# Placing the last context squares ahead of the position-bias table in a fused Perceiver kernel

## Chip, cores and metric

The kernel runs on one core of one Trainium2 chip, as a single launch. The metric is the device time of that launch in microseconds (us), the median of the runs shown.

## What is computed

The reference is a four-level Perceiver: an activation x of 16 batches x 64 tokens x 256 features goes through twelve residual blocks, several of which attend to a context of 16 x 1601 rows of 256 features. Cut to the blocks around the change:

```python
x = x + _L0_attn_ref(_layernorm(x), ...)           # 4 encoder layers, linear attention
x = x + _L0_ffn_ref(_layernorm(x), ...)            # 8 experts, two per token, capacity 160
x = x + _L1_xattn_ref(_layernorm(x), ctx_1024, ...)
...
x = x + _L3_attn_ref(_layernorm(x), ..., L3_attn_rel_emb)

# _L0_ffn_ref
probs = softmax(x @ gate_w.T); top2_w, top2_idx = top_k(probs, 2)
h = relu(einsum('th,ehf->tef', x, W1) + b1); y = einsum('teh,ehf->tef', h, W2) + b2
# _L1_xattn_ref
Pn = ctx * rsqrt(mean(ctx * ctx, -1) + eps) * input_norm_w
# _L3_attn_ref
att = q @ k.T / sqrt(D) + rel_emb[buckets]         # then causal mask, softmax
```

Three pieces of this meet at the change: the **squares** (the sums of squares of the context rows, which only the cross-attention of level 1 needs), the **routes** (which two experts each token goes to, and its place in the expert's table), and the **position bias** (a table of 128 x 1024 values that only the last attention of the kernel needs).

## The kernel before

The program is written in Python with a tile framework that turns tile accesses into semaphore waits. Each engine runs its own instruction list in order. Where `keep_in_program_order` is called (through the wrapper `Written`, line 51, and through `mm` and `tr`, lines 2617 and 2630, while `pinned` is set), the list has the order of the source. A tile that takes over the memory of an earlier tile waits until the last reader of that memory is done (pools with `reuse_waits="tile"`).

`l0_attn` works on the 1024 tokens as two halves, a and b, of four 128-token tiles; its steps are generators that are advanced by hand with `go`. The squares are such a generator as well: `context_squares` (line 2635) loads the context in 48 pieces from the queue of ScalarE (ACT) and emits one `Square` activation with a row sum per 128 x 256 block, 208 in all. `squares(n)` (line 515) emits the next n of them; they are sprinkled through the feed-forward layers, and `squares(999)` emits whatever is left. By then every piece has been loaded and 8 squares are left.

At the end of `l0_attn` (lines 971 to 1008) stand, in this order:

- four calls of `route` (line 836). Each transposes a pair of token tiles, copies them on ACT into `hT`, computes the gate logits on TensorE (PE), ranks them on VectorE (DVE), and has GpSimd (POOL) scatter the token rows into the DRAM table `taken` with four indirect DMAs (line 894). The fourth call, line 983, has nothing beside it.
- the position bias (lines 984 to 1004): 8 matmuls that put the causal mask into PSUM, 128 small matmuls of one-hot bucket rows with the embedding, which finish the tile `pb`, and 16 copies on ACT from `pb` to `kept`. Line 1006 writes the table to DRAM from POOL's queue.
- the rest of the squares (line 1007).

`l0_ffn` (line 1028) comes next. On the queue of SyncE (SP) stand, in order: 8 loads of 256 KB with the weights of experts 4 to 7 (line 1057, into tiles `w12` that take over memory of `l0_attn`), 4 loads of the row of `b2` (line 1062), the first load of gathered tokens `xs` from `taken` (line 1066), 4 loads of `xw` (line 1069), and the other 3 loads of `xs`. The first of the weight loads goes to memory in which the context pieces lay. The first `xs` load waits for all 16 scatters. PE then transposes `xs` and `xw` (`turn`, line 1071), DVE and ACT copy the result to `xsT` (lines 127 and 129), and the experts run: `hidden`, `out`.

DVE and ACT have other work ahead of these copies. DVE: `rms` (line 1214, which reads all the sums of squares), part of the gate softmax (L447), two steps on `rr` (L1216, L1217) and the rest of the softmax (L449 to L451). ACT: the square root of `rms` (L1215), a table load and the softmax's exponential (L448).

Of the kernel before, what the change touches and what calls it, by code (L numbers as in the profile page):

```python
# [64 lines left out]
class Sections:  # L65
# [415 lines left out]
    def l0_attn(self):  # L481
# [25 lines left out]
        with ExitStack() as ctx:  # L507
# [7 lines left out]
            def squares(n):  # L515
                for _ in range(n):
                    next(pieces, None)
# [31 lines left out]
            def norm(s, src, p):  # L549

                mv, r = s.by[p]
                V.reciprocal(r, r)
                for j in range(2):
                    t = 2 * p + j
                    V.tensor_scalar(s.n[:, t, :], src[:, t, :], mv[:, j, 0:1], r[:, j : j + 1], ALU.subtract, ALU.mult)
# [225 lines left out]
            def go(it, n=99):  # L781
                for _ in range(n):
                    if next(it, self) is self:
                        break
# [196 lines left out]
            measure(b, b.x, 1)  # L981
            norm(b, b.x, 1)
            go(route(b, 1))
            banks = ps_kv.tile([P, 2, 512], F32, tag="kv", name="pb")
            banks = [banks[:, 0], banks[:, 1], *(ps.tile([P, 512], F32, tag="tr", name="pb", bufs=2) for _ in range(2))]
            above = self.c("above")
# [17 lines left out]
                        A.copy(to[:, j], of)  # L1004
            self.position_bias = tc.dram_tile([P, 16 * S], F32, name="position_bias")
            nc.gpsimd.dma_start(self.position_bias, bias.rearrange("p r g s -> p (r g s)"))
            squares(999)
            self.pinned = False
        self.at_once.close()

# [1989 lines left out]
```

## Time and profile before

| what | value |
|---|---|
| median of 3 runs (lowest, highest) | 3731.08 us (3728.47, 3732.46) |
| profiled execution: its own time | 3730.16 us |
| profiled execution: span from first to last instruction | 3728.4 us |
| PE busy (matmul) / ACT busy / DVE busy, share of the span | 94% / 39% / 53% |
| mean granted PE clock | 0.979 |
| the 16 copies pb to kept on ACT | start 1343.49, together 3.47 us |
| the 8 last squares on ACT, with their 8 reads of the sum | 1346.99 to 1350.29 us |
| first weight load of line 1057 issued on SP | 1350.31 us |
| first expert matmul (hidden) on PE | 1364.72 us |

All times inside the execution are in microseconds from the start of the span. In a timeline row the columns are: start, duration, engine, source line, operation, output and inputs, shapes, count, and in brackets how long the engine had been idle and what released it. A line of a helper appears for many operations: L59 is the wrapper `Written`, L2619 the matmul helper, L2631 the transpose helper. SPq is the DMA-issuing queue of SP. A row "A <- B" among the waits says that A stood idle until B was done. PEclk is the clock that the TensorE was granted, as a share of full speed.

### The profile page before, as it was taken

What the parts mean: (1) busy time and instruction counts of PE and PEld (TensorE: products, weight loads), DVE (VectorE), ACT (ScalarE), POOL (GpSimd) and SP (SyncE); (2) the same over time, 40 slices, a digit from 0 to 9 for tenths busy, and PEclk for the clock granted to TensorE, in tenths of its full rate; (3) what the DMA queues carried; (4) which work ended last, traced back from release to release, by engine and by line L of the source; (5) the groups of instructions that cost most, each with busy time, mean ns of one, the idle gap of its engine ahead of it and who ended that gap; (6) DMA issues with size and microseconds to landing.
All of it is one profiled execution on the core that took longest, in us unless ns stands there. A gap on an engine that the chain in (4) does not pass through costs nothing.

```text
span 3728.4 us, 71203 instructions
## 1 busy us (share of the span) xinstructions
PE 3499.4 (94%) x31177; PEld 2200.2 (59%) x31192; DVE 1970.9 (53%) x3645; ACT 1461.2 (39%) x2093; POOL 1286.4 (35%) x784
## 2 busy tenths in 40 slices
PE   9999999998999979999988989999999889999997
PEld 4555555564665655555555666667767655555554
DVE  5344333436555635655656555577767765333445
ACT  2333333333444413444433443466666612111123
POOL 2555555552101113433422100577777630000002
PEclk9999999999999979999999999999999989999998
DMA  4111001101333345442101001211111004111550
GB/s 146 38 38 38 28 30 38 38 8 50 101 93 97 116 133 170 147 147 85 64 26 41 1 6 41 72 57 38 57 38 38 11 2 175 36 41 33 241 214 13
DMA packets 108071, 259.77 MB, mean 70 GB/s; under 512 B 9609, under 2 KB 76172, under 8 KB 105456
## 3 DMA queue, kind: packets, MB, share of 16 engines
q1 hardware_dynamic: 99040, 223.14, 16.8%
q10 hardware_dynamic: 6912, 27.27, 2.3%
q0 software_dynamic: 1808, 4.80, 0.5%
q8 instruction: 245, 4.01, 0.4%
q14 instruction: 66, 0.54, 0.0%
HBM read 248.85 MB, written 6.33 MB: 68 GB/s over the span
## 4 chain that ended last, share of the span: by engine, by line
PE 75%; DVE 13%; ACT 7%; issue 2%; DMA 1%; POOL 0%; SPq 0%; ACTq 0%; DVEq 0%; POOLq 0%
PE sc L2619 15%; PE pk L2619 15%; PE lin L2619 6%; PE acc L2619 6%; PE lin_t L2619 5%; ACT e L358 5%; PE pu L2619 4%; PE gate L2166 3%; PE up L2166 3%; PE lin L216 3%; PE pc L1786 3%; PE prz L2619 2%; PE gelu_t L1700 2%; PE turn L2631 1%; PE pa L2619 1%
## 5 line engine op out<-in xcount | busy, mean ns | idle before, releaser
L2548 POOL TENSOR_TENSOR tot<-tot,e 128x1024 f32<-128x1024 f32 (+1 forms) x340 | 803.2, 2362 | 373.3 <-ACT e L358 251.0
L299 DVE TENSOR_REDUCE m<-sc 128x4 f32<-128x2048 f32 x96 | 220.1, 2293 | 271.3 <-PE sc L2619 270.2
L1929 DVE SCALAR_TENSOR_TENSOR e<-sc,row_L_xattn_nbias,free 128x2048 f32<-128x2048 f32 x104 | 244.3, 2349 | 115.5 <-PE sc L2619 113.1
L1931 ACT ACTIVATE e<-e 128x2048 f32<-128x2048 f32 x104 | 198.7, 1911 | 245.8 <-DVE e L1929 245.8
L358 ACT ACTIVATE e<-sc 128x2048 f32<-128x2048 f32 x104 | 195.2, 1877 | 237.3 <-PE sc L2619 235.7
L2619 PE MATMUL sc<-qb,kT 32*128 32x128 f32 x6656 | 245.0, 283 | 36.2 <-DVE m L313 12.3
L2619 PEld LDWEIGHTS sc<-qb,kT 32*128 32x128 f32 x6656 | 206.1, 187 | 80.6 <-issue 22.4
L2619 PEld LDWEIGHTS acc<-e,v 128*32 128x32 f32 x6656 | 169.7, 109 | 105.3 <-issue 96.0
L2619 PE MATMUL acc<-e,v 128*32 128x128 f32 x6656 | 225.9, 276 | 4.7 <-ACT e L1932 4.7
L2619 PE MATMUL pk<-wv,cT 128*128 128x256 f32 x832 | 209.8, 394 | 0.0
L2619 PE MATMUL pk<-cT,wk 128*128 128x512 f32 (+1 forms) x512 | 206.2, 531 | 3.6 <-DVE rows L329 3.6
L1932 ACT ACTIVATE e<-e 128x2048 f32<-128x2048 f32 x104 | 198.7, 1911 | 3.2
L2619 PE MATMUL pk<-wkv,cT 128*128 128x256 f32 x832 | 196.3, 386 | 0.0
L2619 PE MATMUL pk<-cT,wkv 128*128 128x512 f32 (+1 forms) x512 | 194.9, 522 | 0.0
L2619 PEld LDWEIGHTS pk<-wv,cT 128*128 128x128 f32 x832 | 149.5, 190 | 76.4 <-issue 58.9
L2619 PEld LDWEIGHTS pk<-wkv,cT 128*128 128x128 f32 x832 | 153.2, 190 | 28.5 <-issue 4.3
L1786 PE MATMUL pc<-ew,eh 128*128 128x256 f32 x640 | 156.1, 386 | 0.0
L2170 ACT ACTIVATE g<-gate 128x512 f32<-128x512 f32 x68 | 40.6, 597 | 293.4 <-PE gate L2166 293.4
L2619 PE MATMUL sc<-kT,qb 32*128 32x512 f32 (+2 forms) x1536 | 138.9, 461 | 13.8 <-DVE m L299 2.3
L1319 POOL TENSOR_TENSOR e<-e,mx 128x512 f32<-128x512 f32 x96 | 81.9, 885 | 194.3 <-DVE mx L1318 194.3
L2619 PE MATMUL pu<-cn,e 128*64 128x257 f32 (+1 forms) x1248 | 141.6, 381 | 3.3 <-DMA cn<-in_ctx_n 1.8
L2171 DVE TENSOR_TENSOR hT<-up,g 128x512 f32<-128x512 f32 x68 | 47.0, 691 | 183.2 <-PE up L2166 183.2
(544 smaller groups left out, 6425.2 us busy)
## 6 DMA issues: line engine op xcount, KB each, us to landing
cT<-in_ctx_t SPq DMA_DIRECT2D x128, 832.0 KB, 6.4
cn<-in_ctx_n SPq DMA_DIRECT2D x32, 1664.0 KB, 11.9
piece<-in_ctx_n ACTq DMA_DIRECT2D x32, 640.0 KB, 3.9
w<-in_L_attn_W SPq DMA_DIRECT2D x8, 1024.0 KB, 7.0
piece<-in_ctx_n ACTq DMA_DIRECT2D x16, 384.0 KB, 3.7
w<-in_L_ffn_W SPq DMA_DIRECT2D x16, 256.0 KB, 3.1
down<-in_L_ffn_w_down SPq DMA_DIRECT2D x16, 256.0 KB, 2.8
gate<-in_L_ffn_w_gate SPq DMA_DIRECT2D x16, 256.0 KB, 2.7
```

The lines of the kernel that those rows point to most:

```text
L216: nc.tensor.matmul(pm, xT[:, k, t * P : (t + 1) * P], w[:, k, :], start=(k == 0), stop=(k == kc - 1))
L299: nc.vector.tensor_reduce(x.m4[:, g, :, i], pm, AX.X, ALU.max)
L358: nc.scalar.activation(e, pm, AF.Exp, scale=0.25)
L1319: pin(nc.gpsimd.tensor_tensor(p.e, p.e, p.mx.unsqueeze(2).to_broadcast(p.shape), ALU.subtract))
L1700: nc.tensor.matmul(pm, w[:, c, lo : lo + m], cT[:, c, :], start=(c == 0), stop=(c == nk - 1))
L1786: nc.tensor.matmul(pc[:, n, j, :], s.eh[i][:, c, tok], ew2[:, c, cols], start=False, stop=(c == 3))
L1929: nc.vector.scalar_tensor_tensor(e16, pm16, nb, free[:, at : at + P].unsqueeze(1).to_broadcast([P, 16, P]), ALU.add, ALU.mult)
L1931: nc.scalar.activation(e, e, AF.Relu)
L1932: nc.scalar.activation(e, e, AF.Square)
L2166: nc.tensor.matmul(pm[-1], w[:, k, n * P : (n + 1) * P], xT[:, k, tok], start=(k == 0), stop=(k == KC - 1))
L2548: nc.gpsimd.tensor_tensor(tot[:w], x.first if c == 1 else tot[:w], e[:w], ALU.add)
L2619: ins = self.nc.tensor.matmul(*args, **kw)
```

## The change

The call `squares(999)` moves from behind the position bias's write to DRAM to directly behind the last route, in front of the position bias's first matmul. No operation is added or removed.

```diff
             measure(b, b.x, 1)
             norm(b, b.x, 1)
             go(route(b, 1))
+            squares(999)
             banks = ps_kv.tile([P, 2, 512], F32, tag="kv", name="pb")
...
                         A.copy(to[:, j], of)
             self.position_bias = tc.dram_tile([P, 16 * S], F32, name="position_bias")
             nc.gpsimd.dma_start(self.position_bias, bias.rearrange("p r g s -> p (r g s)"))
-            squares(999)
             self.pinned = False
```

In the built program the order of instructions on PE, DVE and SP is the same in both kernels, and on POOL too. On ACT the 8 squares stand directly behind the copy to `hT` of the last route and ahead of the 16 copies from `pb`; before, they stand behind these copies. The wait of SP's first weight load and that of `rms` on DVE is in both kernels for the last square; in ACT's count of finished instructions its number goes from 746 to 730, which is the 16 copies.

## Prediction

> **What bounds the kernel now.** The page says that PE is busy for 94% of the span, so only a place where PE stands still can give much. I looked first for the longest wait of PE around the change. The list of waits from 1326 to 1366 us begins so (total, times, longest):
>
> ```profile
> PE tr L2631 <- DMA xs<-taken: 18.8, 1, 18.8
> DVE rms L1214 <- ACT junk L59: 15.8, 1, 15.8
> ACT kept L59 <- PE pb L2619: 15.4, 1, 15.4
> ```
>
> PE idles 18.8 us before the first transpose of `l0_ffn`; ACT idles 15.4 us before the 16 copies from `pb`. Both idle times lie in one chain, which the timeline of ACT shows:
>
> ```profile
> 1327.46 0.59 ACT L59 COPY hT<-tr 128x512 f32<-128x512 f32 x1 [1.61 <-PE tr L2631]
> 1343.49 3.47 ACT L59 COPY kept<-pb 64x128 f32<-64x128 f32 x16 [15.44 <-PE pb L2619]
> 1346.99 0.42 ACT L59 ACTIVATE junk<-piece 128x256 bf16<-128x256 f32 x1
> ...
> 1350.10 0.19 ACT L59 ACTIVATION_READ_ACCUMULATOR junk<-piece 128x1 f32 x1
> 1350.68 0.38 ACT L1215 ACTIVATE rms<-rms 128x208 f32<-128x208 f32 x1 [0.40 <-DVE rms L1214]
> ```
>
> The squares (`junk`) run from 1346.99 to 1350.29, behind copies that wait for PE. Then SP's queue, which has issued nothing since 1311.65:
>
> ```profile
> 1350.31 4.12 SPq L1057 DMA_DIRECT2D w<-in_L_ffn_W  x8
> 1354.47 1.95 SPq L1062 DMA_DIRECT2D b2w<-in_L_ffn_b  x4
> 1356.89 0.38 SPq L1066 DMA_DIRECT2D xs<-taken  x1
> 1357.55 3.35 SPq L1069 DMA_DIRECT2D xw<-taken  x4
> ```
>
> SP's first weight load goes out 0.02 us after the last square, because it takes over the memory of the context pieces. The gathered tokens `xs` stand behind it in the queue, and PE waits for these. So the end of the squares starts the whole feed-forward. PE around it:
>
> ```profile
> 1336.43 7.03 PE L2619 MATMUL pb<-kept 32*128 32x16 f32 x128
> 1362.26 1.08 PE L2631 MATMUL tr<-cst,xs 128*128 128x128 f32 x4 [18.81 <-DMA xs<-taken]
> 1363.14 1.06 PE L2631 MATMUL tr<-cst,xw 128*128 128x128 f32 x4
> 1364.72 2.50 PE L2619 MATMUL hidden<-xsT,w 128*128 128x160 f32 x8 [0.52 <-DVE xsT L127]
> ```
>
> The first `hidden` at 1364.72 is the point whose shift I work out: from there to 1394 PE has no gap of note.
>
> **The squares on ACT, moved.** Eight squares and their reads took 1350.29 - 1346.99 = 3.30 us. Their data is there: the last piece load was issued at 1294.9, and a piece took at most 5.6 us to land. So they can start when the copy to `hT` ends at 1328.05, and end at about 1331.37. They issue no DMA. The copies behind them cannot start before 1343.49 (end of `pb`), 12.1 us later, so the squares cost nothing there; without that wait they would cost 3.30 us. The copies still end at 1346.96.
>
> **What the squares release.** SP: the 8 weight loads start at about 1331.4, with the 4 of `b2w` behind them by about 1338. The first `xs` stood 6.58 us behind the first weight load (1356.89 - 1350.31), which would be 1338.0, but it also reads the scatter table: the last scatter is issued at 1338.37 and landed 3.0 us later, 1341.4. That wait is new as the last one; behind it on SP stand 4 `xw` and 3 `xs`. The first `xs` took 5.2 us to land, the others down to 2.9. In the same stretch before, the weight loads were still moving, so I take the median of the `xs` loads, 3.4: 1344.8. The four `xw` need 4 issues of about 0.49 (the three `xs` loads took 1.46 us), last at about 1343.3, and 3.0 (their median) to land: 1346.3. Two transposes of 1.08 and 0.98 us: PE would be done by about 1347.4. The PSUM tile of the first transpose is free after half of the copies, about 1345.2, inside that.
>
> DVE and ACT: `rms` (L1214) on DVE runs at 1334.5 instead of 1350.32, right behind the reduction in front of it. But L1215 on ACT stays behind the 16 copies, and so do L448 and all of DVE behind L1216. This chain starts at 1350.68 in the trace and its last step, L451, ends at 1353.24 + 0.22 = 1353.46: 2.78 us. In the changed kernel it starts behind the last copy, 1346.98, and ends at 1349.76.
>
> **What is late next.** The first copy to `xsT` needs the transposes (1347.4) and DVE free (1349.76). DVE is later by 2.4 us. Two DVE copies of 0.42 with a step of about 0.44 follow, since both transposes are done, against 0.86 apart before (1363.38 and 1364.24). `hidden` starts 0.48 after the second copy starts: 1349.80 + 0.44 + 0.48 = 1350.7. The shift is 1364.72 - 1350.7 = **14.0 us**.
>
> **From there to the end.** The later `xs` loads would land by about 1348.5; weights are there. All that SP issues behind waits for PE or DVE steps of the feed-forward (`wq` at 1367.25, the tables `given`, the context loads from 1391.86), and so does POOL's gather at 1390.79: all shift with it. The next stretch that DMA bounds, 1394 to 1425 (busy share 0.99), begins with loads issued at 1391.86 and later, so it shifts whole. The position bias's write goes out at 1347.3 as before.
>
> **Two rules weighed.** First PE's clock:
>
> ```profile
> 1332.70:1343.50 10.80, 10.75 (x137) 9.46 (x137) 1.36 (x9) 0.01 (x1) 3.87 (x4) 0.50 0.15 50
> 1343.50:1362.20 18.70, 0.00 (x0) 0.00 (x0) 2.68 (x7) 8.58 (x35) 0.60 (x1) 0.50 0.62 183
> 1362.20:1369.00 6.80, 6.22 (x25) 5.82 (x26) 2.06 (x7) 1.51 (x4) 0.00 (x0) 0.50 0.42 139
> 1370.00:1386.00 16.00, 16.00 (x117) 13.79 (x119) 7.55 (x19) 4.77 (x10) 0.00 (x0) 1.00 0.30 92
> ```
>
> (Columns: stretch, its length, busy us and count of PE, weight loads, DVE, ACT and POOL, PEclk, DMA share, GB/s.) The Trainium skill, "TensorE: Matmul & The Clock Gate", Part 1, says that about 3.4 us of sustained matmuls bring the full clock and about as long an idle window takes it away. By this rule `pb`'s 10.8 busy us would leave PE warm, and a shorter gap might keep it so: the 4.7 us of half clock from 1364.7 to 1369.4 would halve, 2.3 us more gain. The row says 0.50 all through `pb`, so there is no warmth to keep, and I take none. The same page calls the window free-running: the clock may return up to one window sooner or later than with the old spacing, +-1.7 us.
>
> Second, the Trainium skill, "DMA: Bandwidth & Descriptors", "Queues, rings and completion order", says that every DMA engine takes turns between the queues that have work. This speaks against the change: 2 MB of weights now cross the engines while the last four scatters do. The trace has no such overlap. From below, a scatter landed in 2.4 to 4.0 us alone; from above, the nearest rows behind the weight loads are 5.5 (`b2w`) and 5.2 (first `xs`). Weights moved from 1351 to about 1358 before, so now until about 1339, and the last scatter goes out at 1338.4; I take its 3.0. With the upper ends: scatter 1343.9, `xs` at 1344.1, last `xw` issued at 1346.1 and landed 4.8 later, transposed by 1352.0, second copy at 1352.0, `hidden` at 1352.5: gain 12.2. At the lower ends (2.4 for the scatter, 2.9 and 2.4 for the loads) nothing more is gained, since DVE ends last.
>
> **The sum.** 14.0 us off the profiled 3730.16 is 3716.2. The median of the runs is 0.92 above it, so 3731.08 - 14.0 = **3717.1**.
>
> **The rivals.**
> - *The loads take DVE's place* (chance 0.08): scatters or `xs` late by more than their slack of 2.4 us. For it: the overlap above. Against: by the medians they have 2.4 us to spare, and by the upper ends the loss is only 1.8. Gain 9 to 13, 3718 to 3722.
> - *Given back* (0.06): the chain downstream holds something that does not move with `hidden`, and the gain is within 0.2% (7.5 us): about 3729. For it: DMA is full from 1394 on. Against: those loads are issued behind PE's steps.
> - *Not moved* is part of this case: if the scheduler had left a wait on the copies. Against: the built order and counts (730).
> - *Slower* (0.03): the whole rest runs 14 us earlier against the free-running clock window, and stages that just stayed warm fall to half clock. One lost window costs 1.7 us; from the ninth (14.0 / 1.7 = 8.2) it is a loss, and from 13 it shows: about 3740. Against: three runs of before differ by 4.0 us in all.
> - *More gain* (0.05): the clock comes back at once, 2 to 4 us: 3713 to 3715.
>
> **How the numbers follow.** The main case has 0.78, at 3717.1, with +-1.7 for the window, 1.8 for the scatters and about 2 for the median of another set of runs: 3713.5 to 3721. The range takes in the late loads and the warmer clock: 3712.5 to 3722, a gain of 9 to 18.6. A measurement of this kernel can tell about 0.2%, 7.5 us, from no change. Faster by more than that: 0.78 + 0.08 + 0.05 = 0.91; within: 0.06; slower: 0.03.
>
> **What would show it.** Squares on ACT at 1328 to 1331.4; SP's first weight load at 1331.4; first `xs` issued at about 1341.4, behind the last scatter; copies from `pb` still at 1343.5; `xsT` at about 1349.8, released by DVE's L451 rather than by `xs`; `hidden` at 1350.7; gather on POOL at 1376.8. I am wrong if `xsT` waits for `xs` or `xw` at 1351 or later, if the weight load still goes out behind the copies, or if `hidden` is 14 us early and the end is not.

## The result, and the profile after

| | before | after |
|---|---|---|
| median of 7 runs (lowest, highest), us | 3731.08 (3726.53, 3736.25) | 3719.81 (3713.27, 3723.34) |
| ratio of after to before, 95% interval | | 0.997 (0.9961 to 0.998) |
| profiled execution: own time, span, mean PE clock | 3730.16, 3728.4, 0.979 | 3714.01, 3712.2, 0.981 |
| first `hidden` on PE | 1364.72 | 1351.24 |

Three more sets of runs of the unedited changed kernel (after_again, after_third and after_fourth below) gave ratios of 0.9966, 0.9957 and 0.9964. Every set is below 1 by 0.3 to 0.4%; in medians the four gains are 11.3, 14.6, 14.8 and 14.7 us. The forecast was 14.0.

First the waits from 1326 to 1366 in the profile after (total, times, longest):

```profile
DVE rr L1216 <- ACT rms L1215: 9.5, 1, 9.5
...
PE tr L2631 <- DMA xs<-taken: 8.7, 1, 8.7
ACT kept L59 <- PE pb L2619: 8.3, 1, 8.3
```

PE's wait ahead of the feed-forward went from 18.8 to 8.7 us. Next ACT and SP.

The timeline of ACT:

```profile
1327.93 0.58 ACT L59 COPY hT<-tr 128x512 f32<-128x512 f32 x1 [1.61 <-PE tr L2631]
1328.41 0.42 ACT L59 ACTIVATE junk<-piece 128x256 bf16<-128x256 f32 x1
...
1331.52 0.19 ACT L59 ACTIVATION_READ_ACCUMULATOR junk<-piece 128x1 f32 x1
1339.97 3.47 ACT L59 COPY kept<-pb 64x128 f32<-64x128 f32 x16 [8.26 <-PE pb L2619]
1343.46 0.38 ACT L1215 ACTIVATE rms<-rms 128x208 f32<-128x208 f32 x1
```

The timeline of SP:

```profile
1331.73 4.14 SPq L1057 DMA_DIRECT2D w<-in_L_ffn_W  x8
1335.92 2.57 SPq L1062 DMA_DIRECT2D b2w<-in_L_ffn_b  x4
1344.32 0.38 SPq L1066 DMA_DIRECT2D xs<-taken  x1
1344.75 2.28 SPq L1069 DMA_DIRECT2D xw<-taken  x4
```

The squares run in ACT's wait, 1328.41 to 1331.71, in the 3.30 us expected, and SP's first weight load goes out 0.02 us behind them. Then SP stands still from about 1338.5 to 1344.32, where the forecast let it stand to 1341.4. Then PE, and the two DVE rows that matter.

The timeline of PE:

```profile
1335.71 4.24 PE L2619 MATMUL pb<-kept 32*128 32x16 f32 x128
1348.61 1.08 PE L2631 MATMUL tr<-cst,xs 128*128 128x128 f32 x4 [8.66 <-DMA xs<-taken]
1349.61 1.12 PE L2631 MATMUL tr<-cst,xw 128*128 128x128 f32 x4
1351.24 2.50 PE L2619 MATMUL hidden<-xsT,w 128*128 128x160 f32 x8 [0.52 <-DVE xsT L127]
```

The timeline of DVE:

```profile
1346.03 0.22 DVE L451 TENSOR_TENSOR logits<-logits,sm_mx 128x64 f32<-128x64 f32 x1
1349.74 0.42 DVE L127 COPY xsT<-tr 128x256 f32<-128x256 f32 x1 [3.48 <-PE tr L2631]
```

Two things differ from the forecast. `pb` took 4.24 us instead of 7.03, so the copies and the chain behind them ended early: L451, the last step of the gate softmax on DVE, is done at 1346.25. And the first copy to `xsT` waits 3.48 us for PE, not for DVE's own earlier work. The chain that ended last says why (start, duration, what):

```profile
1337.89 6.28 DMA taken<-n,put
...
1344.32 4.16 DMA xs<-taken
...
1348.61 2.12 PE tr L2631 x8
1350.76 0.44 DVE xsT L127
```

The last scatter landed 6.3 us after its issue instead of the 3.0 in the sum, and the first `xs` went out 2.9 us behind the forecast.

This profile alone would say that another chain took over. But its `pb` ran partly at full PE clock. In the profile of the fourth set of the same kernel `pb` ran at half clock, as before the change. Of after_fourth, the timeline of ACT:

```profile
1344.59 3.47 ACT L59 COPY kept<-pb 64x128 f32<-64x128 f32 x16 [11.57 <-PE pb L2619]
```

The timeline of DVE:

```profile
1350.66 0.23 DVE L451 TENSOR_TENSOR logits<-logits,sm_mx 128x64 f32<-128x64 f32 x1
1351.06 0.76 DVE L127 COPY xsT<-tr 128x256 f32<-128x256 f32 x2 [0.18 <-DMA xs<-taken]
```

The timeline of PE:

```profile
1349.42 1.11 PE L2631 MATMUL tr<-cst,xw 128*128 128x128 f32 x4
1351.87 2.50 PE L2619 MATMUL hidden<-xsT,w 128*128 128x160 f32 x8 [1.33 <-DVE xsT L127]
```

Here PE's transposes are over at 1350.53 and L451 at 1350.89; the copies start 0.17 us behind L451. (The row puts that last 0.18 us down to a DMA, and the list of the chain that ended last follows it. The same 0.17 to 0.18 us behind L451 stands there in other runs with other DMAs named, so I read the order of ends and not the name.) DVE ended last, by 0.4 us.

### The profile page after: what moved, and what is told of

It is laid out like the page before. It is cut to its first block, busy times and chain, and to the rows that moved or that the text cites. A ratio compares the mean times of both kernels' runs of the same rounds, so it can differ in the third digit from the quotient of the medians.

```text
span 3712.2 us, 71203 instructions
## 1 busy us (share of the span) xinstructions
PE 3494.7 (94%) x31177; PEld 2198.2 (59%) x31192; DVE 1972.3 (53%) x3645; ACT 1460.7 (39%) x2093; POOL 1285.7 (35%) x784
## 4 chain that ended last, share of the span: by engine, by line
PE 75%; DVE 13%; ACT 7%; issue 2%; DMA 1%; POOL 0%; SPq 0%; ACTq 0%; DVEq 0%; POOLq 0%
PE pk L2619 15%; PE sc L2619 15%; PE lin L2619 6%; PE acc L2619 6%; PE lin_t L2619 5%; ACT e L358 5%; PE pu L2619 4%; PE gate L2166 3%; PE up L2166 3%; PE lin L216 3%; PE pc L1786 3%; PE prz L2619 2%; PE gelu_t L1700 2%; PE turn L2631 1%; PE pa L2619 1%
```

## What the experiments share

The start of a profiled run wanders by up to 3 us, so all places below are counted from one anchor, the start of ACT's copy to `hT` of the last route (1327.46 before, 1327.93 after). "Behind copies" is `hidden` less the start of the copies from `pb`.

| kernel | copies start | first weight load | first xs issued | hidden | hidden behind copies |
|---|---|---|---|---|---|
| before | 16.03 | 22.85 | 29.43 | 37.26 | 21.23 |
| after | 12.04 | 3.80 | 16.39 | 23.31 | 11.27 |
| after_again | 15.37 | 3.81 | 16.67 | 22.64 | 7.27 |
| after_third | 16.22 | 3.80 | 17.04 | 23.50 | 7.28 |
| after_fourth | 15.35 | 3.80 | 16.05 | 22.63 | 7.28 |
| one_square_late | 15.36 | 19.39 | 27.12 | 34.77 | 19.41 |
| bias_on_sp | 16.15 | 20.58 | 29.82 | 37.82 | 21.67 |
| tokens_first_old_squares | 12.23 | 19.06 | 12.99 | 23.20 | 10.97 |
| tokens_first_new_squares | 12.03 | 16.42 | 12.52 | 19.30 | 7.27 |
| tokens_first_new_again | 15.36 | 17.10 | 13.19 | 22.63 | 7.27 |
| late_small_new | 16.44 | 3.81 | 16.61 | 22.22 | 5.78 |
| tokens_first_late_small | 16.14 | 17.12 | 13.21 | 20.41 | 4.27 |

Two of the columns need a word. "First weight load" is that of experts 4 to 7 (L1057). `pb` ran partly at full clock in the three rows with copies at 12.03 to 12.23, and at half clock in the others.

Theory (**release**): the last square frees SP's queue, and this brings the gain; behind it the chain of copies, square root and softmax on ACT and DVE ends last. Rivals: the squares save time by leaving a busy stretch (**work**); the gain comes from the early `rms` on DVE (**DVE**); or scatter and token loads end last (**loads**).

## Experiments

**The unedited kernel again.** 

> The changed kernel once more, to stand on the same chip as the next three. 11 us below the kernel before (3719.8 against 3731.1), if the first comparison was no luck of its runs. By the release theory (SP's first weight load waits for the last square, and the token loads stand behind it) the first expert matmul is near 1351 us. By the clock theory (the gain is a luckier spacing of half-clock stretches) the difference shrinks to under 4 us.

Measured: 3715.76 us (3711.55 to 3720.82, 7 runs) against 3730.38 (28 runs), ratio 0.9966 (0.9954 to 0.9978). In its profile `pb` was at half clock and `hidden` stood 7.27 us behind the start of the copies: the DVE chain ended last. L451 was done at 1352.06 and the first `xsT` copy began at 1352.23, 1.07 us behind the transposes that it reads.

**One square late.**

```diff
-            squares(999)
+            squares(7)
...
-            self.pinned = False
+            squares(999); self.pinned = False
```

> Seven of the eight squares in the new place, one left behind the 16 copies. Release theory: the last square alone counts, so SP's first weight load goes out 0.6 us behind the last copy, the first expert matmul 15.0 us behind it (before: 17.8), and only 2.7 us of the gain are left: 3728. Work theory (what counts is how much of ACT's 3.3 us lies behind the copies): seven eighths of the gain stay, about 10 us: 3721.

Measured: 3728.67 us (13 runs), ratio 0.9994 (0.9985 to 1.0004).

The timeline of ACT:

```profile
1343.05 3.47 ACT L59 COPY kept<-pb 64x128 f32<-64x128 f32 x16 [11.98 <-PE pb L2619]
1346.55 0.42 ACT L59 ACTIVATE junk<-piece 128x256 bf16<-128x256 f32 x1
```

The timeline of SP:

```profile
1347.08 4.81 SPq L1057 DMA_DIRECT2D w<-in_L_ffn_W  x8
```

The timeline of PE:

```profile
1362.46 2.50 PE L2619 MATMUL hidden<-xsT,w 128*128 128x160 f32 x8 [0.52 <-DVE xsT L127]
```

Seven of the eight squares were early, yet the weight load again went out directly behind the one late square, and `hidden` came 2.5 us earlier than before the change (37.26 to 34.77; 2.7 expected). Of these, 0.67 us come from an earlier start of the copies (16.03 to 15.36), so behind the copies 1.8 us were gained and not 2.7. The rival "work" falls: seven eighths of the work was moved and nearly the whole gain was gone. "DVE" doesn't fall by this run, since `rms` waits for the last square too.

**The wait on the copies put back on SP only.** The write of the position bias is issued from SP instead of POOL, so that SP's queue waits for the copies; squares and `rms` stay early.

```diff
-            nc.gpsimd.dma_start(self.position_bias, bias...)
+            nc.sync.dma_start(self.position_bias, bias...)
```

> The changed kernel with one edit: the write of the position bias to DRAM (line 1007) is issued from SP's queue in place of POOL's. It stands there ahead of the weight loads and waits for the 16 copies from pb; the squares stay early, and so does rms on DVE. If SP's queue is the path (release theory), the first weight load goes out 0.4 to 0.9 us behind the last copy, about where one late square put it, the first hidden follows 15 us behind it, and the gain over the kernel before is 2 to 3 us: 3727 to 3728. If the gain came from the early rms on DVE or from the squares leaving the busy stretch (rivals), 3716 to 3720 remains.

Measured: 3732.36 us (13 runs) against 3734.95 (21 runs), ratio 0.9994 (0.9986 to 1.0002).

The timeline of SP:

```profile
1347.55 0.35 SPq L1007 DMA_DIRECT2D position_bias<-kept  x1
1348.48 5.45 SPq L1057 DMA_DIRECT2D w<-in_L_ffn_W  x8
```

The timeline of PE:

```profile
1365.72 2.50 PE L2619 MATMUL hidden<-xsT,w 128*128 128x160 f32 x8 [0.52 <-DVE xsT L127]
```

The timeline of DVE has `rms` early, as in the changed kernel (1333.91 there):

```profile
1334.15 0.26 DVE L1214 TENSOR_SCALAR rms<-ss 128x208 f32<-128x208 f32 x1
```

The first weight load stood 0.96 us behind the last copy (1347.52), just over the expected 0.4 to 0.9. `hidden` stood 17.24 behind that weight load, not 15: first `xs` was issued 9.24 us behind the first weight load, 6.58 before. The table's write now stands on the same queue ahead of both; that it causes this was not tested. So no gain is left in the trace (37.82 against 37.26), and the total does not tell 2.2 us from none. The absolute 3727 to 3728 was missed: the kernel before measured 3734.95 in this set, where the expectation took 3730 to 3731. What the run was for is clear: with `rms` early and all squares early, the gain is gone once SP waits. As the source of the whole gain, "DVE" and "work" fall.

**The queue freed without moving the squares.** The kernel before, with the weight loads of experts 4 to 7 moved behind the token loads on SP.

```diff
-            ws = [weights(e) for e in range(E)]
+            ws = [weights(e) for e in range(E // 2)]
...
                         nc.sync.dma_start(xw[W * r : W * (r + 1)], last(taken, r))
+            ws += [weights(e) for e in range(E // 2, E)]
```

> The kernel before, with the weight loads of experts 4 to 7 moved behind the token loads on SP's queue; squares in the old place. Release theory: the token loads no longer stand behind a wait for the squares; first xs issued at about 1341.4 behind the last scatter, PE's transposes done by 1347.5; then DVE ends last, whose rms still waits for the last square at 1350.3: first copy to xsT at 1353.5, first expert matmul at 1354.4, a gain of 10 of the 14 us: 3721. Work theory: ACT is unchanged, so nothing: 3731. DVE theory (rms on DVE is what the change set free): nothing either, 3731.

Measured: 3719.41 us (13 runs), ratio 0.9973 (0.9965 to 0.9982).

The timeline of SP:

```profile
1341.39 0.38 SPq L1066 DMA_DIRECT2D xs<-taken  x1
...
1347.46 4.22 SPq L1057 DMA_DIRECT2D w<-in_L_ffn_W  x8
```

The timeline of DVE:

```profile
1347.46 0.27 DVE L1214 TENSOR_SCALAR rms<-ss 128x208 f32<-128x208 f32 x1 [12.79 <-ACT junk L59]
...
1350.39 0.23 DVE L451 TENSOR_TENSOR logits<-logits,sm_mx 128x64 f32<-128x64 f32 x1
```

The timeline of PE:

```profile
1345.52 1.12 PE L2631 MATMUL tr<-cst,xw 128*128 128x128 f32 x4
1351.60 2.50 PE L2619 MATMUL hidden<-xsT,w 128*128 128x160 f32 x8 [4.96 <-DVE xsT L127]
```

The squares are where they were, and most of the gain is there: 11.0 us of the 14.6 that the change gave beside it. The weights were not urgent (among PE's waits from 1350 to 1400 there is none for `w`); the tokens queued behind them were. What is missing is the DVE chain: with late squares `hidden` stands 10.97 us behind the copies instead of 7.27, 3.7 us (the 3.30 of the squares, and the 0.4 from `rms` on DVE to L1215). The totals differ by 3.65 us, which sets of 13 and 7 runs with this spread can barely tell from nothing; the trace carries this step. So the release brings the larger part of the gain, and the early `rms` behind the early squares the rest: "DVE" is wrong as a rival for the whole and right for this part.

**Both at once**, run twice. The edit to the loads is the one above, on the changed kernel.

> The changed kernel with the weight loads of experts 4 to 7 behind the token loads. If the late landing of the scatters in the changed kernel (4.2 to 7.6 us, before 2.4 to 4.0) comes from the weight loads beside them, the scatters land in 2.4 to 4.0 us again, the first xs goes out at about 1341 instead of 1344.3, and DVE ends last: first copy to xsT 2.8 us behind the last copy from pb, first expert matmul 3.7 us behind it (1350.7 when pb runs at half clock, 1347.1 at full clock): 1 to 4 us below the changed kernel, 3716 to 3719. If the landing is late for another reason, nothing changes: 3720.

Measured: 3715.6 us (6 runs), ratio 0.9966 (0.9953 to 0.998), the total of after_again. Its profile had `pb` at full clock and `hidden` at 19.30, 4.0 us earlier than the profile after, whose `pb` was alike:

```profile
1348.86 2.50 PE L2619 MATMUL hidden<-xsT,w 128*128 128x160 f32 x8 [1.67 <-DVE xsT L127]
```

The expected 1 to 4 us in the total did not show, so it was repeated. 

> The changed kernel with the weight loads of experts 4 to 7 behind the token loads on SP, a second time, to pool with the first. In the first profile the first hidden stood 19.3 us behind the copy to hT of the last route, against 22.6 to 23.5 in three profiles of the changed kernel. If these 3 to 4 us reach the end, the median lies 3 to 4 us below that of the changed kernel beside it; if they are taken back behind the feed-forward, or show only where pb runs at full clock, the two are within 1.5 us.

Measured: 3717.75 us (9 runs) against 3729.42, ratio 0.9966 (0.9956 to 0.9976).

The timeline of SP:

```profile
1342.31 0.38 SPq L1066 DMA_DIRECT2D xs<-taken  x1
```

The timeline of PE:

```profile
1347.17 1.06 PE L2631 MATMUL tr<-cst,xw 128*128 128x128 f32 x4
1351.75 2.50 PE L2619 MATMUL hidden<-xsT,w 128*128 128x160 f32 x8 [3.53 <-DVE xsT L127]
```

The timeline of DVE:

```profile
1350.54 0.23 DVE L451 TENSOR_TENSOR logits<-logits,sm_mx 128x64 f32<-128x64 f32 x1
1350.94 0.76 DVE L127 COPY xsT<-tr 128x256 f32<-128x256 f32 x2 [0.18 <-DMA w<-in_L_ffn_W]
```

This pair separates "loads" from DVE. With `pb` at half clock the tokens were transposed by 1348.23, L451 ended at 1350.77, and `hidden` stood at 22.63, to 0.01 us where after_fourth has it with its late tokens. Earlier tokens are worth nothing there. When `pb` runs partly at full clock they are worth 4.0 us at `hidden`, by one pair of profiles.

The control beside the repeat. 

> The changed kernel, unedited, on the same chip beside it: 12 to 16 us below the kernel before, as in the three sets of runs so far (ratios 0.997, 0.9966, 0.9957).

Measured: 3714.75 us (5 runs), ratio 0.9964 (0.995 to 0.9978). The reordered kernel stands 3.0 us above this control, where at most 1.5 either way was expected for no gain; the two ratios are 0.9966 and 0.9964 with intervals of 0.002 and more. So the reordering gives no gain in total that these runs can show.

**The DVE chain taken away.** On the changed kernel `rms`, its root, and the first reduction and exponential of the softmax are held at their place in the source, behind the experts' first work.

```diff
-        nc.vector.tensor_reduce(mx, l, AX.X, ALU.max)
+        pin(nc.vector.tensor_reduce(mx, l, AX.X, ALU.max))
...
-            nc.scalar.activation(rms, rms, AF.Sqrt)
+            tc.keep_in_program_order(nc.scalar.activation(rms, rms, AF.Sqrt))
```

> The changed kernel with rms and its square root (lines 1214 and 1215) and the first reduction and the exponential of the gate softmax (lines 446 and 448) held at their place in the source, behind the experts' first work, so that DVE and ACT have nothing ahead of the copies to xsT. Theory of the tie (the DVE chain and the chain of scatter and xs end within 1 us of each other): the first hidden comes 0 to 0.7 us earlier, measured from the copy to hT of the last route, when pb runs at half clock, and not at all when it runs at full clock; the total is that of the changed kernel within 1 us. Rival, the prediction's own step (DVE ends last by 2.4 us): hidden comes 2.4 us earlier, 3713 to 3714.

Measured: 3724.9 us (8 runs) against 3734.95, ratio 0.9963 (0.995 to 0.9976). The total was expected within 1 us of the changed kernel's; the median lies 4.8 us above the 3720.11 of the control below, yet the intervals of the two ratios overlap over most of their length, so it shows neither gain nor loss. `hidden` stood at 22.22, 0.4 to 1.3 us earlier than in the three profiles of the changed kernel with `pb` at half clock. That is a little more than the tie's 0 to 0.7, and less than the 2.4 of the prediction's slack. On DVE's timeline the first copy now waits for PE:

```profile
1349.80 0.42 DVE L127 COPY xsT<-tr 128x256 f32<-128x256 f32 x1 [14.44 <-PE tr L2631]
```

**Both chains taken away.** The two edits above together. 

> The changed kernel with both chains cut: the weight loads of experts 4 to 7 stand behind the token loads on SP, and the small steps of DVE and ACT are held behind the experts' first work. Theory of the tie: only both together move hidden. The scatters then land in 2 to 4 us, the first xs goes out 2.5 to 4 us earlier than in the changed kernel, and hidden starts some 18 us behind the copy to hT, where the changed kernel took 22.1 and 22.7: 4 us earlier whatever PE's clock in pb, 3711 to 3713 for the median. Rival: the small steps pinned behind the experts' first work delay it as much as they are worth, and the total stays at 3715 to 3717.

Measured: 3718.68 us (5 runs), ratio 0.9959 (0.9946 to 0.9972). `hidden` stood at 20.41, 2.2 to 3.1 us earlier than in those three profiles, not 4, because a third chain comes up, as PE's timeline shows:

```profile
1347.67 1.12 PE L2631 MATMUL tr<-cst,xs 128*128 128x128 f32 x4 [1.78 <-ACT kept L59]
```

The first transpose now waits for the copies from `pb`, whose PSUM banks it takes over. The total is that of the control below within the noise and not the expected 3711 to 3713, so no version here is shown to beat the changed kernel.

**The control of that set.** 

> The changed kernel once more, unedited, beside the three others on the same chip. Both theories: 3714 to 3720. In its trace, if pb runs at half clock the first copy to xsT starts behind DVE's last step of the softmax; if pb runs at full clock it starts behind PE's transposes of xs and xw.

Measured: 3720.11 us (5 runs), ratio 0.9957 (0.9945 to 0.997), 14.8 us below the 3734.95 beside it. `pb` ran at half clock throughout, and the first copy to `xsT` began at 1352.12, 0.17 us behind L451; PE's transposes had ended at 1351.60.

## Why the prediction was right, step by step

- *"So the end of the squares starts the whole feed-forward"*: shown. One late square of eight, or SP alone held at the copies, takes nearly all or all of the gain away; SP freed without moving a square brings 11.0 of 14.6 us. The rest is the shorter DVE chain, which the prediction has too (`rms` at 1334.5 instead of 1350.32; 1333.91 measured).
- *Squares at no cost in ACT's wait*: right, 3.30 us; of ACT's wait 11.57 to 12.45 us were left behind them, and 8.26 us where `pb` ran at full clock.
- *"and landed 3.0 us later, 1341.4"*: **this step failed.** From the last scatter's issue to the first `xs` issue it took 6.4, 6.4, 6.8 and 5.8 us in the four profiles of the changed kernel, more than the upper end of 5.5 that the working took from the loads behind the weights. With the weights behind the tokens it took 2.6, 2.8, 2.9 and 3.0. What differs is whether the 2 MB of weights cross the engines meanwhile. The prediction had named this overlap, from the turn-taking of the Trainium skill's "DMA: Bandwidth & Descriptors" ("Queues, rings and completion order"), and still took the figure without it. The page gives no size, and no run here shows whether turns between the queues or another kind of sharing makes the scatters slow.
- *"DVE is later by 2.4 us"*: right engine, wrong size. In the profiles with `pb` at half clock L451 ended 0.35 us (after_third) and 0.36 us (after_fourth) behind PE's transposes; in after_again the second transposes ended 0.33 us behind it, too early to hold up the copies. The late scatter had used up some 2 us of the slack. (A slip in the working adds to this little: the `xw` loads took 2.6 us in the median, not 3.0.) `hidden` came 7.27 to 7.28 us behind the copies; the working has 7.2 (1350.7 - 1343.49).
- *"Copies from `pb` still at 1343.5"*: they start with `pb`'s end, and that is not fixed: 16.03 behind the anchor before, 15.35 to 16.22 in three profiles after, 12.04 in the fourth. There the rival **the loads take DVE's place** held, with a gain of 13.95 us at `hidden`, just outside its 9 to 13: behind the anchor the first `xs` was 2.4 us late (16.39 against 13.94 by the working), all of the slack, and the early end of `pb` took DVE out of the way as well.
- *Hidden at 1350.7*: 23.24 behind the anchor by the working; 22.63, 22.64, 23.31 and 23.50 measured. Two errors, late tokens and a `pb` that sometimes ends 3 to 4 us sooner, hid behind each other because the two chains are nearly tied. That the shift comes so close to 14.0 is in part luck.
- *"All shift with it"*: the gather on POOL came 13.9 us earlier behind the anchor (63.33 to 49.44). In the profiled pair, counted from the start of each span, DVE's steps came 13.6 us earlier at the first `xsT` copy, 14.6 at 1410, 12.3 at 1431 (one PE stage, `pu`, took 7.22 us with a stretch of half clock in it, where it took 5.87 at full clock), 11.4 to 15.4 from there to 3690, and 16.2 at the end. Nothing took the gain back for good. The steps behind `hidden` come and go with stretches of half clock: at 3468 the lead rose from 12.7 to 15.4, and there the kernel before has a clock of 0.50 from 3458.2 to 3465.0 where the profile after passes the same work at 1.00 (3445.5 to 3452.3). I take the 2 us by which the two spans differ more than `hidden` for such stretches; no run tests it.
- *Slower, not moved, given back*: none is seen in any of the four sets.

*No warmth to keep* (the Trainium skill, "TensorE: Matmul & The Clock Gate", Part 1): the half clock behind `hidden` stays. The clock returned in the slice from 1354 to 1356, some 4.7 us behind `hidden`, as before (1364.7 to 1369.4). `pb` itself differs between executions of one kernel. The row of the stretch of `pb` in the profile after, with the columns as before:

```profile
1332.30:1340.00 7.70, 7.65 (x137) 6.59 (x137) 1.70 (x11) 0.03 (x1) 3.87 (x4) 0.72 0.89 264
```

The same for after_fourth:

```profile
1333.80:1344.60 10.80, 10.76 (x137) 9.46 (x137) 1.70 (x11) 0.01 (x1) 3.87 (x4) 0.50 0.84 269
```

In the first, the full clock came after 3.4 us of sustained matmuls, as the page has it, but it lasted from 1335.4 to 1338.8 only and fell to 0.50 while PE was busy without a break. The second has 10.76 busy us at 0.50, where by the page's rule the clock should have come up. So the rule fits neither profile as a whole. Neither case brought more gain at `hidden`.

The traces say more about when it comes up. In each of the twelve profiles all changes of the clock lie on a grid of 3.41 us, whose place against the program differs between executions. (A step at half clock thus costs at most the 1.7 us of the prediction's window.) In three (after, tokens_first_old_squares, tokens_first_new_squares) the 8 mask matmuls ahead of the 128 small ones began 0.27, 0.68 and 0.24 us behind a grid point, and the next grid point brought the full clock for one step of 3.41 us. In the other nine they began 0.75 to 1.55 us behind one, and the clock stayed at half throughout `pb`. That the phase of the grid decides is argued from these twelve and not tested; what is counted over such a step stays open.

Left open too: whether earlier tokens reach the end of the program when `pb` comes up to full clock. In the one pair of profiles they did not. Counted from the start of the span, a `qT` step (L1277) of tokens_first_new_squares came 4.8 us earlier than in the profile after (1427.40 against 1432.17), yet the spans end at 3713.7 and 3712.2. Part of the lead went where tokens_first_new_squares has a clock of 0.50 (3443.1 to 3449.9) and the profile after 1.00.

## What to carry to other kernels

When a transfer queue stands still, look at what its first entry waits for and what is queued behind that entry: here, loads that nobody needed yet waited for a reused buffer and held up the loads that everybody needed. After such a release, work out the ends of all chains that meet at the next step. Here, with `pb` at half clock, two of them ended within 0.4 us of each other; shortening one alone moved `hidden` by 0 to 1.3 us, both by 2.2 to 3.1. A landing time measured alone can be too short once the released transfers run beside it: here 2.4 to 4.0 us became 5.7 to 7.6.

## What the runs showed of the hardware

Indirect scatters landed later beside a bulk stream. The rows give the four scatters of the last route from issue to landing, first of the profile after, with 2 MB of weights moving:

```profile
DMA to landing us min/median/max: 5.9/6.6/7.6
```

And of tokens_first_new_squares, where the weights are issued behind the tokens:

```profile
DMA to landing us min/median/max: 2.4/2.4/3.1
```

The runs of one kernel spread by 10 us (3713.27 to 3723.34), more than the 4.0 us that three runs of before had suggested. The profiled executions go with the granted clock: four profiles of the changed kernel have spans of 3712.2, 3710.8, 3722.9 and 3709.7 us at mean clocks of 0.981, 0.982, 0.978 and 0.982. With five runs the interval of the ratio spans 0.995 to 0.9978, which is 10 us; a step of 3 us needs far more runs, or a place in the trace.

In one set of runs DVE stood idle ahead of the first `qT` (L1277), behind the feed-forward, with no releaser in the core's records: for 3.8, 5.4, 7.5 and 8.5 us in its four profiles (bias_on_sp, tokens_first_late_small, after_third, late_small_new). In the eight profiles of the other sets it was 1.3 to 1.6 us there, with PE as releaser. It lies behind `hidden` and enters no reading of `hidden` above; what share it has in that set's longer times (3734.95 us before the change, 3729.42 to 3731.08 in the others) and what causes it is not known.
